# Batch row 0 of a conditional linear layer before a mixture of experts: loads in halves, another order of the first products and sums

## The chip, the cores and the metric

The kernel runs on one core of a Trainium2 chip. TensorE multiplies matrices, VectorE and ScalarE work elementwise and empty TensorE's result banks (PSUM), GpSimd (POOL) issues the indirect transfers, SyncE (SP) issues the direct ones. The metric is the device time of one execution in microseconds (us), less being better. Before the change it is 971.0 us, the median of three runs between 967.38 and 971.63.

## What is computed

For each of 4 batch rows of 1024 tokens, a linear layer is chosen by a category number. Its result goes through a router that sends each token to one of 8 experts, of 512 places each; each expert is a two-layer network with a ReLU; its output, times the router's probability, is added to x. All data are float32.

```python
def _L0_cond_ref(x, cat_ids, W, b):
    selected_W = W[cat_ids]
    selected_b = b[cat_ids]
    return jnp.einsum('bsd,bdh->bsh', x, selected_W) + selected_b[:, None, :]

def _L0_ffn_ref(x, Wr, W1, W2):
    ...
    probs = jax.nn.softmax(xf.astype(jnp.float32) @ Wr, axis=-1)
    eidx = jnp.argmax(probs, axis=-1)
    ...
    xe = xf[dispatch]
    h = jnp.maximum(jnp.einsum('ecd,edf->ecf', xe, W1), 0.0)
    ye = jnp.einsum('ecf,efd->ecd', h, W2)
    ye = ye * (pe * valid.astype(ye.dtype))[:, :, None]
    ...

x = x + _L0_ffn_ref(_L0_cond_ref(x, itok, W, b), Wr, W1, W2)
```

Here x is (4, 1024, 512), W (64, 512, 512), b (64, 512), Wr (512, 8), W1 (8, 512, 2048), W2 (8, 2048, 512).

## The kernel before

There are two stages. The first runs over the batch rows b = 0 to 3: the chosen linear layer and the router, whose results go to memory (`xc_dram`, and `slots` for the routing). The second runs over the experts, gathering rows by indirect transfers. The change touches the first stage alone, and in it only row 0.

A batch row is two chunks of 512 tokens (chunk c = 2b + g). Each chunk's product of a 512x512 matrix with the 512x512 weights is cut into 2x2 blocks and done with seven block products instead of eight (Strassen's way, as Winograd arranged the sums). The x blocks are called a11 to a22 and need the sums s1 to s4; the weight blocks b11 to b22 need t1 to t4. `linear(b, g, k)` (L400) does product k: 4 matmul instructions, which the trace shows as 8 records. k = 1 is a11 times b11, k = 2 a12 times b21, k = 6 is s2 times t2, 5 is s1 times t1, 7 is s3 times t3, 4 is a22 times t4, 3 is s4 times b22. Products 1, 6, 7 and 4 grow in one PSUM bank "x", which VectorE reads between them (`plus_bias`, L417, into the tiles s1, s6, s7), so that each next product of that bank waits for the reading of the one before.

Ahead of the products stand several helpers:

- `load_x` (L228) and `load_batch` (L193) issue the loads on SP: a chunk of x of 1 MB, the weights `cw` of 1 MB, the bias `cb` spread over the partitions, and the bias once more as columns, `cbt`. The category number is read into a register before (L194).
- `transpose_x` (X, L236) turns 128 rows of x by four TensorE transpositions; ScalarE copies the result from PSUM to `xT`. With a chunk's last rows it gives VectorE the four sums s1 to s4.
- `transpose_w` (WT, L260) does the same with a fourth of the weights into `wT`. These are for the router alone.
- `sum_w` (L221) gives VectorE the four differences t1 to t4.
- `through` (WM, L274) and `through_summed` (WS, L310) multiply the transposed weights with the router's matrix, giving `wrc`; `router` (R, L313) multiplies `xT` with `wrc`, `router_summed` (RS, L328) adds the parts; `choose` and `rank` pick the expert and the place.
- `keep_warm` (L65) issues matmuls on a tile of zeros, so that TensorE is active while loads run.

The order of TensorE and SP is written out by hand (`manual_schedule`): it is the order of the calls. For a row, `ORDER` (L455) lists the 14 products of the two chunks, and the tables `beside` (L463) and `loads` (L509) say which helpers follow each. The order of VectorE and ScalarE is chosen by a scheduler, except where `issue_after` (in `behind`, L73) puts an instruction behind the one kept in `latest`. Each engine works through its own list in order. PSUM for transpositions (`ps_t`) has two buffers.

The stage begins at L520: loads of three chunks of x and three rows' weights, six idle matmul instructions, four X, four WT, and then the loop over rows and products.

Of the kernel before, what the change touches and what calls it, by code (L numbers as in the profile page):

```python
# [11 lines left out]
ALU = mybir.AluOpType  # L12
# [4 lines left out]
P = 128  # L17
# [5 lines left out]
def kernel(  # L23
# [11 lines left out]
    nc = tc.nc  # L35
# [5 lines left out]
    KC = D // P  # L41
    NT = T // P
    GT = S // P
    XT = 4
    CT = XT * P
    HT = CT // 2
    SC = CAP // P
    HK = KC // 2
# [8 lines left out]
    xf = x.rearrange("b s d -> (b s) d")  # L57
# [7 lines left out]
    def keep_warm(pool, n):  # L65

        ps = pool.tile([P, D], F32, tag="t", name="ps_idle")
        for _ in range(n):
            nc.tensor.matmul(ps, lhsT=idle[:, 0:P], rhs=idle, start=True, stop=True)

    latest = [None]
# [6 lines left out]
    def unordered(group, ins):  # L78
# [14 lines left out]
        out=wr_sb[:, :, 0:E], in_=wr.rearrange("(kc p) e -> p kc e", p=P)  # L93
# [43 lines left out]
    banks = {}  # L137
# [40 lines left out]
    with (  # L178
# [14 lines left out]
        def load_batch(b):  # L193
            n = nc.sync.value_load(cat_sb[0:1, b : b + 1], min_val=0, max_val=NCAT - 1)  # L194
            w = cwp.tile([P, KC, D], F32, tag="cw", bufs=3, name=f"cw_{b}")
            nc.sync.dma_start(
                out=w,
                in_=cond_w[bass.ds(n, 1), :, :].rearrange("o (kc p) h -> p (o kc) h", p=P),
            )
            bias = cwp.tile([P, D], F32, tag="cb", bufs=3, name=f"cb_{b}")  # L200
            nc.sync.dma_start(
                out=bias, in_=cond_b[bass.ds(n, 1), :].to_broadcast([P, D])
            )
            bias_t = cwp.tile([P, KC], F32, tag="cbt", bufs=3, name=f"cbt_{b}")
            nc.sync.dma_start(
                out=bias_t, in_=cond_b[bass.ds(n, 1), :].rearrange("o (kc p) -> p (o kc)", p=P)
            )

            b11, b12, b21, b22 = (
                w[:, i * HK : (i + 1) * HK, j * HD : (j + 1) * HD]  # L210
                for i in range(2)
                for j in range(2)
            )
            wd = cwp.tile([P, 4, HK, HD], F32, tag="wd", name=f"wd_{b}")
            t1, t2, t3, t4 = (wd[:, k, :, :] for k in range(4))
            later_sums[b] = (b11, b12, b21, b22, t1, t2, t3, t4)
            cond[b] = (w, bias, bias_t, {1: b11, 2: b21, 3: b22, 4: t4, 5: t1, 6: t2, 7: t3})

        later_sums = {}
# [7 lines left out]

        def load_x(c):  # L228
            t = xin.tile([P, XT, D], F32, tag="x", name=f"x_{c}")
            nc.sync.dma_start(  # L230
                out=t,
                in_=xf[c * CT : (c + 1) * CT, :].rearrange("(j p) d -> p j d", p=P),
            )
            xrows[c] = t

        def transpose_x(b, i):  # L236


            c, j = b * 2 + i // XT, i % XT
            if j == 0:  # L240
                xT[c] = xtp.tile([P, KC, CT], F32, tag="xT", name=f"xT_{c}")
            ps = ps_t.tile([P, KC, P], F32, tag="t", name=f"ps_xT_{c}_{j}")
            for kc in range(KC):
                nc.tensor.transpose(ps[:, kc, :], xrows[c][:, j, kc * P : (kc + 1) * P], ident)
            nc.scalar.copy(xT[c][:, :, j * P : (j + 1) * P], ps)
            if j == XT - 1:
                a11, a12, a21, a22 = (
                    xT[c][:, k * HK : (k + 1) * HK, half * HT : (half + 1) * HT]
                    for half in range(2)
                    for k in range(2)  # L250
                )
                t = xsp.tile([P, 4, HK, HT], F32, tag="xs", name=f"xs_{c}")
                s1, s2, s3, s4 = (t[:, k, :, :] for k in range(4))
                nc.vector.tensor_tensor(s1, a21, a22, ALU.add)
                nc.vector.tensor_tensor(s2, s1, a11, ALU.subtract)
                nc.vector.tensor_tensor(s3, a11, a21, ALU.subtract)
                nc.vector.tensor_tensor(s4, a12, s2, ALU.subtract)
                xS[c] = {1: a11, 2: a12, 3: s4, 4: a22, 5: s1, 6: s2, 7: s3}

        def transpose_w(b, hc):  # L260
            if hc == 0:
                wT[b] = wtp.tile([P, KC, D], F32, tag="wT", name=f"wT_{b}")
            ps = ps_t.tile([P, KC, P], F32, tag="t", name=f"ps_wT_{b}_{hc}")
            for kc in range(KC):
                nc.tensor.transpose(
                    ps[:, kc, :], cond[b][0][:, kc, hc * P : (hc + 1) * P], ident
                )
            nc.scalar.copy(wT[b][:, hc, :].rearrange("p (k n) -> p k n", n=P), ps)
# [131 lines left out]
        def linear(b, g, k):  # L400

            key = ("lin", b, g)
            c = b * 2 + g
            ps = bank(ps_x, key, k, [P, 2, HD], "xc", bufs=2 if BANK[k] == "x" else 1)
            _, bias, _, right = cond[b]
            for j in range(2):
                for kc in range(HK):
                    nc.tensor.matmul(
                        ps[:, j, :],
                        lhsT=xS[c][k][:, kc, j * P : (j + 1) * P],  # L410
                        rhs=right[k][:, kc, :],
                        start=(k in OPENS and j == 0 and kc == 0),
                        stop=(k == LAST[BANK[k]] and j == 1 and kc == HK - 1),
                        skip_group_check=True,
                    )

            def plus_bias(into, half):  # L417
                nc.vector.tensor_tensor(
                    into,
                    ps,  # L420
                    bias[:, half * HD : (half + 1) * HD].unsqueeze(1).to_broadcast([P, 2, HD]),
                    ALU.add,
                )

            def block(i, j):
                return xco.tile([P, 2, HD], F32, tag=f"c{i}{j}", name=f"xc{i}{j}_{c}")

            def done(t, i, j):
                at = c * CT + i * HT
                nc.sync.dma_start(  # L430
                    out=xc_dram[at : at + HT, j * HD : (j + 1) * HD].rearrange(
                        "(j p) d -> p j d", p=P
                    ),
                    in_=t,
                )

            if k in (1, 6, 7):
                banks[key, k] = parts.tile([P, 2, HD], F32, tag=f"s{k}", name=f"s{k}_{b}_{g}")
                plus_bias(banks[key, k], 0 if k == 1 else 1)
            if k in (2, 3):  # L440
                t = block(0, int(k == 3))
                latest[0] = nc.vector.tensor_tensor(
                    t, ps, banks.pop((key, 1 if k == 2 else 6)), ALU.add
                )
                done(t, 0, int(k == 3))
            if k == 7:
                t = block(1, 1)
                nc.vector.tensor_tensor(t, banks[key, "y"], banks.pop((key, 7)), ALU.add)
                done(t, 1, 1)
            if k == 4:  # L450
                t = block(1, 0)
                plus_bias(t, 0)
                done(t, 1, 0)
# [5 lines left out]
        )  # L459

        X, WT, WM, WS = transpose_x, transpose_w, through, through_summed
        R, RS = router, router_summed
        beside = {  # L463
            (0, 0): [(sum_w, 0), (WM, 0)],
            (0, 1): [(X, 0, 4), (X, 0, 5), (WS, 0)],
            (0, 2): [(X, 0, 6), (X, 0, 7), (R, 0, 0)],
            (0, 3): [(WT, 1, 0)],
            (0, 4): [(WT, 1, 1), (RS, 0, 0)],
            (0, 5): [(WT, 1, 2), (R, 0, 1)],
            (0, 6): [(WT, 1, 3)],  # L470
            (0, 7): [(X, 1, 0), (WM, 1), (RS, 0, 1), (choose, 0)],
            (0, 8): [(X, 1, 1), (behind, sum_w, 1)],
# [47 lines left out]
        with tc.manual_schedule(engines={mybir.EngineType.PE, mybir.EngineType.SP}):  # L520
            load_x(0)
            load_batch(0)
            load_x(1)
            load_batch(1)
            load_x(2)
            load_batch(2)
            keep_warm(ps_t, 6)
            for i in range(XT):
                transpose_x(0, i)
            for hc in range(KC):  # L530
                transpose_w(0, hc)
            for b in range(B):
                for i, (g, k) in enumerate(ORDER):
                    linear(b, g, k)
                    for f, *at in loads.get((b, i), []) + beside.get((b, i), []):
                        f(*at)
            keep_warm(ps_t, 7)

        nc.scalar.dma_start(
            out=table.rearrange("p e c r -> p e (c r)"),  # L540
            in_=slots.rearrange("(e p c) r -> p e (c r)", e=E, c=SC),
# [237 lines left out]
```

## Time and profile before

| what | us |
|---|---|
| three runs: lowest, median, highest | 967.38, 971.0, 971.63 |
| the profiled execution: its time | 969.31 |
| its span, from first to last instruction | 967.5 |
| busy in the span: TensorE, VectorE, ScalarE, GpSimd | 950.1, 472.7, 171.0, 139.1 |
| first transposition of x on TensorE, from the span's start | 8.53 |
| first product on TensorE | 13.45 |
| idle matmuls at the end of the first stage begin | 153.27 |
| first transposition of the second stage | 160.80 |

Sections of the profile that are used here: the timeline gives, for a run of like instructions, the start and length in us, the engine, the line, output and inputs with their shapes, the number of records and in brackets the idle time before them and who ended it. PE is TensorE, PEld its weight loads, DVE VectorE, ACT ScalarE. A float32 matmul instruction shows as two records. The answer by windows gives for each stretch its length and each engine's busy time, then the granted clock of TensorE, the share of the DMA engines and the GB/s moved. The waits give an engine and line, whom it waited for, and the us in total, the times and the longest.

### The profile page before, as it was taken

Reading aid. Unit: us, or ns where it says so; the run is one execution under the profiler, and the core shown is the slowest. Engines: PE = TensorE matmul, PEld = TensorE weight load, DVE = VectorE, ACT = ScalarE, POOL = GpSimd, SP = SyncE. Lnnn points to the kernel's source line nnn. Section 1 sums busy time; section 2 is a strip of 40 time slices with the busy share of each in tenths; the row PEclk is TensorE's granted clock in tenths of the full one; section 3 lists DMA queues with packets and bytes.
Section 4 is the critical chain, followed back from the end, with each engine's and each line's share of the span. In section 5 each row is a group of like instructions: output and inputs, shape, how many; then the busy total and the mean of one; then the engine's idle time right before and its main releaser. Section 6 shows DMA issues by size and latency. Waiting matters only on the chain.

```text
span 967.5 us, 11249 instructions
## 1 busy us (share of the span) xinstructions
PE 950.1 (98%) x4570; PEld 812.2 (84%) x4570; DVE 472.7 (49%) x822; ACT 171.0 (18%) x289; POOL 139.1 (14%) x141
## 2 busy tenths in 40 slices
PE   9999988999999999999999999999999999999997
PEld 5788776888888888888888888888888888888886
DVE  4656574374337522762276317731673157325621
ACT  3233200320023002310231013101320132003200
POOL 0043332200022001200130013001300130012001
PEclk9999998999999999999999999999999999999999
DMA  9389223399134313532253225313532352332001
GB/s 323 115 166 227 90 81 93 132 400 337 60 131 159 131 55 114 173 107 74 84 175 127 82 93 174 130 48 128 174 101 73 127 174 71 104 126 87 1 0 44
DMA packets 95509, 123.18 MB, mean 127 GB/s; under 512 B 8820, under 2 KB 82548, under 8 KB 95266
## 3 DMA queue, kind: packets, MB, share of 16 engines
q1 hardware_dynamic: 85042, 97.54, 31.6%
q0 software_dynamic: 8704, 24.85, 7.8%
q8 instruction: 36, 0.59, 0.2%
q10 hardware_dynamic: 1712, 0.08, 0.1%
q14 instruction: 15, 0.12, 0.1%
HBM read 105.96 MB, written 25.23 MB: 136 GB/s over the span
## 4 chain that ended last, share of the span: by engine, by line
PE 58%; issue 17%; DVE 4%; DMA 2%; POOL 1%; SPq 1%; POOLq 0%; ACT 0%; DVEq 0%
PE hx L630 17%; PE yx L673 16%; PE yy L673 9%; PE hy L630 8%; PE hz L630 4%; PE yz L673 3%; DMA w_b<-in_L_ffn_W_dram 2%; PE ps_e L607 1%; POOL out_dram L694 1%; POOL rows L583 1%; SPq L566 1%; DMA rows<-xc_dram,src_row 0%; DVE h L150 0%; DVE h L151 0%; DVE h L149 0%
## 5 line engine op out<-in xcount | busy, mean ns | idle before, releaser
L630 PE MATMUL hx<-xe,w 128*128 128x256 f32 x1024 | 242.8, 382 | 1.4 <-ACT s L643 1.4
L630 PEld LDWEIGHTS hx<-xe,w 128*128 128x128 f32 x1024 | 195.3, 192 | 27.6 <-ACT s L643 1.8
L643 ACT COPY s<-hx 128x512 f32<-128x512 f32 x96 | 55.9, 582 | 437.7 <-PE hx L630 437.7
L630 PE MATMUL hy<-xe,w 128*128 128x256 f32 x512 | 122.1, 380 | 0.0
L673 PE MATMUL yx<-w_t,h 128*128 128x256 f32 x512 | 119.9, 380 | 1.2 <-DVE rows L667 1.2
L673 PE MATMUL yx<-w_b,h 128*128 128x256 f32 x512 | 116.6, 381 | 1.1 <-DVE rows L667 1.1
L694 POOL DMA_INDIRECT out_dram<-rows,dst_row x32 | 31.9, 998 | 572.1 <-DVE rows L667 572.1
L673 PEld LDWEIGHTS yx<-w_b,h 128*128 128x128 f32 x512 | 95.8, 190 | 16.5 <-DVE rows L667 3.7
L673 PEld LDWEIGHTS yx<-w_t,h 128*128 128x128 f32 x512 | 95.4, 190 | 15.9 <-DVE rows L667 2.0
L630 PEld LDWEIGHTS hy<-xe,w 128*128 128x128 f32 x512 | 97.4, 190 | 13.3 <-DVE h L646 0.4
L667 DVE SCALAR_TENSOR_TENSOR rows<-yx,table,rows 128x256 f32<-128x256 f32 x64 | 31.0, 484 | 140.2 <-PE yx L673 140.2
L647 ACT ACTIVATE h<-h 128x512 f32<-128x512 f32 x96 | 60.5, 630 | 203.0 <-DVE h L646 203.0
L646 DVE TENSOR_TENSOR h<-hy,s 128x512 f32<-128x512 f32 x64 | 44.2, 691 | 98.8 <-PE hy L630 54.8
L630 PE MATMUL hz<-xe,w 128*128 128x256 f32 x256 | 61.7, 380 | 0.0
L673 PE MATMUL yz<-w_b,h 128*128 128x256 f32 x256 | 58.7, 383 | 0.4
L673 PE MATMUL yy<-w_b,h 128*128 128x256 f32 x256 | 58.4, 381 | 0.0
L673 PE MATMUL yy<-w_t,h 128*128 128x256 f32 x256 | 57.9, 380 | 0.0
L583 POOL DMA_INDIRECT rows<-in_x_dram,at x32 | 40.2, 1257 | 122.7 <-DVE at L594 93.0
L673 PEld LDWEIGHTS yz<-w_b,h 128*128 128x128 f32 x256 | 48.1, 190 | 9.5 <-DVE rows L667 3.4
L630 PEld LDWEIGHTS hz<-xe,w 128*128 128x128 f32 x256 | 48.9, 191 | 6.6
L673 PEld LDWEIGHTS yy<-w_b,h 128*128 128x128 f32 x256 | 47.6, 190 | 8.1 <-DVE rows L667 1.4
L673 PEld LDWEIGHTS yy<-w_t,h 128*128 128x128 f32 x256 | 48.2, 190 | 6.2
(118 smaller groups left out, 894.7 us busy)
## 6 DMA issues: line engine op xcount, KB each, us to landing
w<-in_L_ffn_W_dram SPq DMA_DIRECT2D x64, 512.0 KB, 4.3
w_b<-in_L_ffn_W_dram SPq DMA_DIRECT2D x32, 1024.0 KB, 5.5
x<-in_x_dram SPq DMA_DIRECT2D x8, 1024.0 KB, 9.7
xc_dram<-xc SPq DMA_DIRECT2D x32, 256.0 KB, 4.1
out_dram<-in_x_dram SPq DMA_DIRECT2D x2, 2816.0 KB, 22.4
cw<-in_L_cond_W_dram SPq DMA_DIRECT2D x4, 1024.0 KB, 11.2
out_dram<-in_x_dram SPq DMA_DIRECT2D x1, 2560.0 KB, 16.0
cb<-in_L_cond_b_dram SPq DMA_DIRECT2D x4, 256.0 KB, 9.9
```

Source lines behind the costliest of these rows:

```text
L566: nc.sync.dma_start(out=t[k], in_=w2[e, i * F // 2 : (i + 1) * F // 2, j * D // 2 : (j + 1) * D // 2].rearrange("(m p) d -> p m d", p=P),)
L583: nc.gpsimd.indirect_dma_start(out=into[n], out_offset=None, in_=source, in_offset=bass.IndirectOffsetOnAxis(ap=at[:, c : c + 1], axis=0),)
L607: nc.tensor.transpose(ps[:, kc, :], r[:, kc * P : (kc + 1) * P], ident)
L630: nc.tensor.matmul(ps[:, j, :], lhsT=w1s[e, g][:, LEFT[k], kc, j * P : (j + 1) * P], rhs=xes[e][:, RIGHT1[k], kc, :], start=(k in OPENS an ...
L643: nc.scalar.copy(banks[key, k], ps)
L646: latest[0] = nc.vector.tensor_tensor(into, ps, part, ALU.add)
L647: nc.scalar.activation(into, into, AF.Relu)
L667: nc.vector.scalar_tensor_tensor(row, ps[:, at, :], table[:, e, half * HC + at, 0:1], row, ALU.mult, ALU.add)
L673: nc.tensor.matmul(ps[:, at, :], lhsT=hs[e, m // HB][:, LEFT[k], m % HB, at * P : (at + 1) * P], rhs=w2s[e][RIGHT2[k]][:, m, :], start=(k ...
L694: nc.gpsimd.indirect_dma_start(out=of, out_offset=bass.IndirectOffsetOnAxis(ap=dst_row[:, n : n + 1], axis=0), in_=residual.pop(n), in_off ...
```

## The change

For chunk 0, x is loaded by two transfers of 512 KB each, and for row 0 so are the weights; all other loads stay whole. Three idle matmul instructions are issued instead of six. Row 0's four WT leave their place ahead of the loop and stand behind its first and second product; the helpers that followed the products 0 to 5 of row 0 are spread anew. VectorE's eight sums of chunk 0 get an order by hand: s1, t1, s2, t2, then the reading of product 1's bank, then s3, t3, s4, t4 (`rest_of_first`). For this, `plus_bias` returns its instruction, and `latest` is also set behind product 1. From product 4 of chunk 0 on (index 6 of the order), TensorE's list is the one before, and the lists of the other engines are so from about there on.

```diff
--- before.py
+++ after.py
@@ -193,10 +193,14 @@
         def load_batch(b):
             n = nc.sync.value_load(cat_sb[0:1, b : b + 1], min_val=0, max_val=NCAT - 1)
             w = cwp.tile([P, KC, D], F32, tag="cw", bufs=3, name=f"cw_{b}")
-            nc.sync.dma_start(
-                out=w,
-                in_=cond_w[bass.ds(n, 1), :, :].rearrange("o (kc p) h -> p (o kc) h", p=P),
-            )
+            kcs = [(0, HK), (HK, KC)] if b == 0 else [(0, KC)]
+            for i, (lo, hi) in enumerate(kcs):
+                nc.sync.dma_start(
+                    out=w[:, lo:hi, :],
+                    in_=cond_w[bass.ds(n, 1), lo * P : hi * P, :].rearrange(
+                        "o (kc p) h -> p (o kc) h", p=P
+                    ),
+                )
             bias = cwp.tile([P, D], F32, tag="cb", bufs=3, name=f"cb_{b}")
             nc.sync.dma_start(
                 out=bias, in_=cond_b[bass.ds(n, 1), :].to_broadcast([P, D])
@@ -227,11 +231,23 @@
 
         def load_x(c):
             t = xin.tile([P, XT, D], F32, tag="x", name=f"x_{c}")
-            nc.sync.dma_start(
-                out=t,
-                in_=xf[c * CT : (c + 1) * CT, :].rearrange("(j p) d -> p j d", p=P),
-            )
+            n = XT // 2 if c == 0 else XT
+            for j in range(0, XT, n):
+                nc.sync.dma_start(
+                    out=t[:, j : j + n, :],
+                    in_=xf[c * CT + j * P : c * CT + (j + n) * P, :].rearrange(
+                        "(j p) d -> p j d", p=P
+                    ),
+                )
             xrows[c] = t
+
+        def behind_this(f):
+            with tc.issue_after(latest[0].ins):
+                latest[0] = f()
+
+        def rest_of_first():
+            for f in later_sums.pop("rest"):
+                behind_this(f)
 
         def transpose_x(b, i):
 
@@ -251,10 +267,28 @@
                 )
                 t = xsp.tile([P, 4, HK, HT], F32, tag="xs", name=f"xs_{c}")
                 s1, s2, s3, s4 = (t[:, k, :, :] for k in range(4))
-                nc.vector.tensor_tensor(s1, a21, a22, ALU.add)
-                nc.vector.tensor_tensor(s2, s1, a11, ALU.subtract)
-                nc.vector.tensor_tensor(s3, a11, a21, ALU.subtract)
-                nc.vector.tensor_tensor(s4, a12, s2, ALU.subtract)
+                tt = nc.vector.tensor_tensor
+                todo = [
+                    lambda: tt(s1, a21, a22, ALU.add),
+                    lambda: tt(s2, s1, a11, ALU.subtract),
+                    lambda: tt(s3, a11, a21, ALU.subtract),
+                    lambda: tt(s4, a12, s2, ALU.subtract),
+                ]
+                if c == 0:
+
+                    b11, b12, b21, b22, t1, t2, t3, t4 = later_sums.pop(0)
+                    todo[1:1] = [lambda: tt(t1, b12, b11, ALU.subtract)]
+                    todo[3:3] = [lambda: tt(t2, b22, t1, ALU.subtract)]
+                    todo[5:5] = [lambda: tt(t3, b22, b12, ALU.subtract)]
+                    todo[7:7] = [lambda: tt(t4, b21, t2, ALU.subtract)]
+                    rest = todo[4:]
+                    latest[0] = todo[0]()
+                    for f in todo[1:4]:
+                        behind_this(f)
+                    later_sums["rest"] = rest
+                else:
+                    for f in todo:
+                        f()
                 xS[c] = {1: a11, 2: a12, 3: s4, 4: a22, 5: s1, 6: s2, 7: s3}
 
         def transpose_w(b, hc):
@@ -415,7 +449,7 @@
                     )
 
             def plus_bias(into, half):
-                nc.vector.tensor_tensor(
+                return nc.vector.tensor_tensor(
                     into,
                     ps,
                     bias[:, half * HD : (half + 1) * HD].unsqueeze(1).to_broadcast([P, 2, HD]),
@@ -436,7 +470,9 @@
 
             if k in (1, 6, 7):
                 banks[key, k] = parts.tile([P, 2, HD], F32, tag=f"s{k}", name=f"s{k}_{b}_{g}")
-                plus_bias(banks[key, k], 0 if k == 1 else 1)
+                evicted = plus_bias(banks[key, k], 0 if k == 1 else 1)
+                if k == 1:
+                    latest[0] = evicted
             if k in (2, 3):
                 t = block(0, int(k == 3))
                 latest[0] = nc.vector.tensor_tensor(
@@ -461,12 +497,12 @@
         X, WT, WM, WS = transpose_x, transpose_w, through, through_summed
         R, RS = router, router_summed
         beside = {
-            (0, 0): [(sum_w, 0), (WM, 0)],
-            (0, 1): [(X, 0, 4), (X, 0, 5), (WS, 0)],
-            (0, 2): [(X, 0, 6), (X, 0, 7), (R, 0, 0)],
-            (0, 3): [(WT, 1, 0)],
-            (0, 4): [(WT, 1, 1), (RS, 0, 0)],
-            (0, 5): [(WT, 1, 2), (R, 0, 1)],
+            (0, 0): [(rest_of_first,), (WT, 0, 0), (WT, 0, 1)],
+            (0, 1): [(WT, 0, 2), (WT, 0, 3)],
+            (0, 2): [(WM, 0), (X, 0, 4), (X, 0, 5)],
+            (0, 3): [(X, 0, 6), (WS, 0), (X, 0, 7)],
+            (0, 4): [(R, 0, 0), (WT, 1, 0), (WT, 1, 1)],
+            (0, 5): [(R, 0, 1), (WT, 1, 2), (RS, 0, 0)],
             (0, 6): [(WT, 1, 3)],
             (0, 7): [(X, 1, 0), (WM, 1), (RS, 0, 1), (choose, 0)],
             (0, 8): [(X, 1, 1), (behind, sum_w, 1)],
@@ -524,11 +560,9 @@
             load_batch(1)
             load_x(2)
             load_batch(2)
-            keep_warm(ps_t, 6)
+            keep_warm(ps_t, 3)
             for i in range(XT):
                 transpose_x(0, i)
-            for hc in range(KC):
-                transpose_w(0, hc)
             for b in range(B):
                 for i, (g, k) in enumerate(ORDER):
                     linear(b, g, k)
```

## The prediction

> **What bounds the kernel now.** I read the page first. TensorE is busy 98% of 967.5 us and the chain that ended last is mostly PE; the expert loop, four fifths of the span, is not touched. So I went to the only place where the change acts, the first 35 us, in the timeline of TensorE, to see when its useful work starts and where it stalls.
>
> ```profile
> 1.45 7.24 PE L69 MATMUL ps_idle<-idle 128*128 128x512 f32 x12 [1.45 <-DVE idle L89]
> ...
> 8.53 1.04 PE L244 MATMUL ps_xT<-ident,x 128*128 128x128 f32 x8
> 9.80 1.14 PE L244 MATMUL ps_xT<-ident,x 128*128 128x128 f32 x8 [0.24 <-ACT xT L245]
> 11.13 1.15 PE L265 MATMUL ps_wT<-ident,cw 128*128 128x128 f32 x8 [0.19 <-ACT xT L245]
> 12.46 1.15 PE L265 MATMUL ps_wT<-ident,cw 128*128 128x128 f32 x8 [0.18 <-ACT wT L268]
> ...
> 28.00 1.89 PE L408 MATMUL xcx_lin<-cw,xT 128*128 128x256 f32 x8
> 29.73 0.60 PE L265 MATMUL ps_wT<-ident,cw 128*128 128x128 f32 x4
> 30.26 1.06 PE L317 MATMUL ps_lT<-xT,wrc 128*32 128x512 f32 x8
> 31.26 2.00 PE L408 MATMUL xcx_lin<-wd,xT 128*128 128x256 f32 x8
> ```
>
> The reader sees three things. Twelve idle matmul records (six instructions, two records each) hold TensorE until 8.53. Then 32 transposition records run in groups of eight, 1.27 to 1.33 us apart, because each group waits for ScalarE to empty a bank; the same four-instruction transposition between products takes 0.44 to 0.53 (29.73 to 30.26). From 13.45, where the first product starts, TensorE has no gap up to 31.26, where product 4 of the first chunk starts (index 6 of the order). That start is my measuring mark: both kernels have done the same set of work by then.
>
> Next, when the operands land: the answer by tile, narrowed to one issue each, for x and then for the weights cw, with issue lengths in ns, first and last start in us, and the time from issue to landing.
>
> ```profile
> L230 SPq DMA_DIRECT2D x<-in_x_dram x1: 422/422/422, 1.1 to 1.1; - x1
> ...
> DMA to landing us min/median/max: 5.9/5.9/5.9
> ```
>
> ```profile
> L196 SPq DMA_DIRECT2D cw<-in_L_cond_W_dram x1: 392/392/392, 2.9 to 2.9; - x1
> ...
> DMA to landing us min/median/max: 7.2/7.2/7.2
> ```
>
> x is issued at 1.14 and lands at about 7.0, 1.5 us before TensorE turns to it: the idle matmuls, not x, set the start. The weights, issued at 2.92, land at 10.1; VectorE's first sum starts at 10.12 and confirms it. The windows of the same time show how fast the bytes come (last two columns: share of the DMA engines and GB/s):
>
> ```profile
> 4.00:6.00 2.00, 2.00 (x5) 0.83 (x4) 0.00 (x0) 0.00 (x0) 0.00 (x0) 1.00 1.01 314
> 6.00:8.00 2.00, 2.00 (x6) 0.91 (x5) 0.00 (x0) 0.00 (x0) 0.00 (x0) 1.00 1.02 307
> 8.00:10.00 2.00, 1.76 (x12) 1.14 (x11) 0.00 (x0) 0.84 (x2) 0.00 (x0) 1.00 0.98 367
> ```
>
> The DMA engines are full; halves come sooner only because they stand first in line. Last, the waits of TensorE over 0 to 170 us:
>
> ```profile
> PE ps_e L607 <- DMA rows<-xc_dram,src_row: 2.5, 3, 1.4
> PE xcx_lin L408 <- DVE s L418: 1.5, 1, 1.5
> PE ps_idle L69 <- DVE idle L89: 1.5, 1, 1.5
> PE rk L375 <- DVE past L356: 1.5, 1, 1.5
> ```
>
> Nothing there waits for a load from memory except the gathers at 160 us, which themselves follow the last product. So whatever the start gains runs through to the end.
>
> **What the Trainium skill says.** "TensorE: Matmul & The Clock Gate", Part 1: the clock is halved until about 3.4 us of activity have passed, and falls again after an idle window. The trace agrees: weight loads of idle matmuls stand 0.85 us apart until 5.03 and 0.43 afterwards, 3.6 us after the first. Part 4 says that transpositions don't count as activity; here the trace differs: 4.9 us of nothing else (8.53 to 13.45) did not cool the clock, as the next products run at 0.22 us per record. "DMA: Bandwidth & Descriptors", Queues, rings and completion order: each DMA engine takes descriptors in ring order; the trace agrees (x at 7.0, cw at 10.1, the second x at 4.78 + 9.0 = 13.8, in order of issue). The same page, on why a DMA increments its semaphore by 16: only the full count says that data has landed, so half a tile can be used early only as a transfer of its own. No run here shows that yet.
>
> **The change part by part.**
>
> Three idle instructions fewer: 6 records x 0.43 = 2.58 us. The idle work ends at 8.53 - 2.58 = 5.95, if the first half of x is there. Half of x is 0.52 MB, 1.67 us at 314 GB/s, so it lands near 7.0 - 1.7 = 5.4. Bounds: 4.5 to 6.5; I take 5.4, no wait.
>
> x transpositions: chunk rows 0 and 1 from 5.95; rows 2 and 3 from 5.95 + 1.27 = 7.22, which both the ScalarE copy and the second half of x (7.0, with the extra issue perhaps 7.4) allow. TensorE is free at about 8.2 to 8.4.
>
> First product: needs only the upper half of cw. 0.52 MB at 367 GB/s is 1.43 us, so it lands at 10.12 - 1.43 = 8.7; I take 8.8 for the second x issue ahead of it. TensorE waits about 0.5 us. Bounds: 8.2 (TensorE free) and 10.1 (halves land together).
>
> The weight transpositions move from ahead of the first product to behind the first two. Four groups at 0.5 in the flow are 2.0 us. The path from first product to mark was 31.26 - 13.45 = 17.81; now it is 17.81 + 2.0 = 19.8. The mark comes at 8.8 + 19.8 = 28.6, against 31.26: **2.6 us gained**. Bounds: 3.2 from 8.2, 1.3 from 10.1. The router steps only change places between the same products, their sum stays.
>
> VectorE in order of use: its eight sums, 0.6 to 0.72 us apart, are the same eight. s1 starts when the fourth copy of xT ends (5.95 + 3.03 = 9.0), t1 at 9.6, s2 at 10.3, t2 at 10.9 (second half of cw at about 10.2), eviction of product 1 at 11.6 to 12.3. Product 6 needs t2, s2 and that eviction; it stands at 8.8 + 1.8 + 0.9 + 1.8 + 0.9 = 14.2. Cover: 1.9 us, and beyond that each us of lateness costs one. The other four sums (12.3 to 15) sit behind the eviction by hand; product 7 needs s3 and t3 only near 21. The first result block's addition waits to about 15; its store is waited for by the next chunk's block at about 40. So the order costs nothing but is what lets product 6 follow; s3 and t3 ahead of the eviction would have eaten 1.3 of the cover.
>
> SP issues two more transfers, 0.42 and 0.39 us and some register work: the bias goes out up to 1.0 later and lands by 10.7 + 1.0 = 11.7, about when the eviction reaches it. The second x lands by 14.8 instead of 13.8, used at about 17; the second cw is issued at 6.22 and the slowest of the first three took 11.8, so 19 at the latest, used by TensorE near 24. Covered by 2 and 5 us. No DMA volume is added.
>
> Sum against the profiled execution: 969.3 (967.5 of span and 1.8 around it) - 2.6 = 966.7. The runs shown have their median at 971.0, 1.7 higher; scaled to them, 971.0 - 2.6 = **968.4 us**, 0.27% less. What a measurement here can tell from no change is about 0.5%, 4.9 us: the expected gain is real but below it.
>
> **The rivals.**
>
> Halves land together. For it: the DMA engines are full from 4 us, and two transfers interleaved finish near each other. Against: ring order above. Gain 1.3, or 0.4 if the extra issue adds 0.9: 970.1.
>
> Gain and luck at the stage boundary. Between 162.4 and 168.8 the windows show the granted clock at 0.50: the gap before the gathers cools TensorE. If the shift changes which window that gap falls in, up to 3 us more go: 968.4 - 3 = 965.4, which would read as faster. Nothing says that it does; the runs before differ by 4.3 us, so something of this size varies anyway.
>
> A cold clock at the start, the slower side. Where: the wait ahead of the first product at 8.4. With three idle instructions less, transpositions that leave gaps and a wait of 0.5 to 1.7 us, TensorE could fall to half clock. Price from the boundary: 6.4 us at 0.50, 3.2 us lost. From the likely gain that gives 971.0 - 2.6 + 3.2 = 971.6; with halves together (gain 0.4), 973.8. It decides once the lost time exceeds 2.6: over 5.2 us at half clock. Against it: the 4.9 us of transpositions with gaps of 0.2 that stayed warm. Passing 0.5% slower needs two such stretches or a first half of cw after 16 us.
>
> The gain doesn't arrive: DMA stays full until 28 us in absolute time, so a load waited for then would hold TensorE to the old clock time. Covers of 2 to 5 us speak against it. 971.0.
>
> **How the numbers follow.** Forecast 0.62; halves together 0.15; boundary luck 0.12; cold start 0.08; nothing arrives 0.03. Faster by over 0.5%: the luck case and a little of the forecast's edge, 0.14. Slower by over 0.5%: the worse half of the cold start, 0.04. Same: 0.82. The range runs from 965.0 (luck) to 971.5 (nothing gained or a cold start at its usual price), leaving out under 2 in 10.
>
> **What would show it.** Right: TensorE's first x transposition near 6.0, the first product near 8.8 with a short wait, no wait of product 6 for VectorE, and the mark (product 4 of chunk 0) near 28.6; the last idle matmuls of the conditional stage then begin 2.6 us sooner than 153.27. Wrong: the first product after 10; a TensorE wait on VectorE between 12 and 25; products spaced 0.43 per record before 20 us; or a mark at 28.6 with the end of the stage where it was.

## The result, and the profile after

Six runs of the changed kernel lie between 965.1 and 967.78 us, median 966.1; six of the kernel before have their median at 970.9. The ratio is 0.9957, with a 95% interval of 0.9938 to 0.9975: 4.2 us faster (2.4 to 6.0), where 2.6 were forecast; the two medians are 4.9 apart. The time stands inside the range given. The profiled execution took 965.1 us with a span of 963.3, against 969.3 and 967.5.

The timeline of TensorE in the kernel after, the lines that answer to those of before (start, length, line, what, records, and in brackets the idle time before and who ended it):

```profile
1.45 4.75 PE L69 MATMUL ps_idle<-idle 128*128 128x512 f32 x6 [1.45 <-DVE idle L89]
6.03 1.04 PE L260 MATMUL ps_xT<-ident,x 128*128 128x128 f32 x8
7.31 1.15 PE L260 MATMUL ps_xT<-ident,x 128*128 128x128 f32 x8 [0.24 <-ACT xT L261]
8.97 1.99 PE L442 MATMUL xcx_lin<-cw,xT 128*128 128x256 f32 x8 [0.51 <-DMA cw<-in_L_cond_W_dram]
10.80 1.04 PE L299 MATMUL ps_wT<-ident,cw 128*128 128x128 f32 x8
11.67 1.89 PE L442 MATMUL xcz_lin<-cw,xT 128*128 128x256 f32 x8
13.40 1.04 PE L299 MATMUL ps_wT<-ident,cw 128*128 128x128 f32 x8
14.27 1.89 PE L442 MATMUL xcx_lin<-wd,xs 128*128 128x256 f32 x8
...
28.59 1.89 PE L442 MATMUL xcx_lin<-wd,xT 128*128 128x256 f32 x8
```

The first product starts at 8.97 instead of 13.45, the weights' four transpositions stand behind the first two products (two in each row of 8 records), and the mark (the last line) comes at 28.59 instead of 31.26. The only wait on a load in these lines is the 0.51 ahead of the first product. The third product of the list (k = 6, at 14.27) follows without a wait for VectorE, whose own timeline shows why: s1, t1, s2 and t2 are done at 11.6 and the reading of the first bank at 12.2.

```profile
9.11 0.69 DVE L272 TENSOR_TENSOR xs<-xT 128x512 f32<-128x512 f32 x1 [6.61 <-ACT xT L261]
9.72 0.68 DVE L280 TENSOR_TENSOR wd<-cw 128x512 f32<-128x512 f32 x1
10.32 0.69 DVE L273 TENSOR_TENSOR xs<-xs,xT 128x512 f32<-128x512 f32 x1
10.92 0.69 DVE L281 TENSOR_TENSOR wd<-cw,wd 128x512 f32<-128x512 f32 x1
11.52 0.69 DVE L452 TENSOR_TENSOR s<-xcx_lin,cb 128x512 f32<-128x512 f32 x1
```

How the gain then travels, from the timelines of the two profiled executions. In the second stage hx, hy and hz are the PSUM banks of an expert's first layer, yx and yz those of its second; w1 and w2 are the weights of the two layers (w and w_b in the traces). The stretch between the end of the first stage and the first product hz, in which TensorE waits for gathered rows, is called the gap below.

| moment, us from the span's start | before | after | gained by then |
|---|---|---|---|
| mark, product 4 of chunk 0 | 31.26 | 28.59 | 2.67 |
| idle matmuls at the end of the first stage | 153.27 | 150.50 | 2.77 |
| first transposition of gathered rows | 160.80 | 157.97 | 2.83 |
| first product hz of expert 0 | 168.90 | 163.88 | 5.02 |
| first product yx of expert 0 | 214.03 | 209.84 | 4.19 |
| end of the span | 967.5 | 963.3 | 4.2 |

The start gives 2.7 and keeps them for 130 us. Then 2.2 more come inside the gap, between the first gathered transposition and hz (8.1 us apart before, 5.9 after), and 0.8 are given back by yx. The windows of the gap start where the idle matmuls end, at 159.44 and 156.67; first the kernel before, then after (the last three columns are the granted clock of TensorE, the share of the DMA engines and GB/s):

```profile
159.44:163.44 4.00, 1.77 (x9) 1.13 (x8) 0.69 (x1) 0.00 (x0) 2.11 (x3) 0.84 0.68 202
163.44:167.44 4.00, 3.69 (x13) 3.25 (x14) 2.21 (x4) 0.00 (x0) 0.00 (x0) 0.50 0.12 46
```

```profile
156.67:160.67 4.00, 1.31 (x9) 0.84 (x8) 1.12 (x2) 0.00 (x0) 2.00 (x3) 1.00 0.69 197
160.67:164.67 4.00, 3.61 (x20) 3.04 (x21) 2.76 (x5) 0.58 (x1) 0.00 (x0) 1.00 0.13 49
```

Waiting for the gathered rows left TensorE idle for more than half of the first four microseconds in both, yet the clock fell to half in one and stayed in the other, which was idle for longer. What was given back is in the waits of TensorE from 160 to 225 us, in the kernel after:

```profile
PE hx L664 <- ACT s L677: 1.4, 1, 1.4
PE ps_e L641 <- DMA rows<-xc_dram,src_row: 0.9, 2, 0.7
PE hy L664 <- DVE h L680: 0.7, 1, 0.7
PE yx L707 <- DVE rows L701: 0.5, 1, 0.5
```

The wait of hy is new. The kernel before has the 1.4 and the 0.5 as well. VectorE's timeline says what stands behind the new one; the first line is of the kernel before, the other two of the kernel after:

```profile
203.48 1.23 DVE L156 TENSOR_TENSOR w_t<-w_b,w_b 128x1024 f32<-128x1024 f32 x1 [2.80 <-DMA w_b<-in_L_ffn_W_dram]
...
199.29 1.23 DVE L156 TENSOR_TENSOR w_t<-w_b,w_b 128x1024 f32<-128x1024 f32 x1 [3.53 <-DMA w_b<-in_L_ffn_W_dram]
200.44 0.68 DVE L680 TENSOR_TENSOR h<-hy,s 128x512 f32<-128x512 f32 x1
```

A sum of w2 blocks waits 3.53 for its load, and the sum h that empties TensorE's bank is queued behind it. SP had issued these loads only at 179.06, behind a load of w1 that itself waits for a buffer. In the kernel before they went out at 183.97, so the issue moved forward by 4.9, nearly as much as TensorE; but the sum that needs them moved by only 4.2. The loads took 0.7 longer, and why is open.

### The profile page after: what moved, and what is told of

Read it like the earlier page. It is cut to its first block, busy times and chain, and to the rows that moved or that the text cites. A ratio compares the mean times of both kernels' runs of the same rounds, so it can differ in the third digit from the quotient of the medians.

```text
span 963.3 us, 11240 instructions
## 1 busy us (share of the span) xinstructions
PE 944.5 (98%) x4564; PEld 807.2 (84%) x4564; DVE 471.9 (49%) x822; ACT 170.7 (18%) x289; POOL 140.3 (15%) x141
## 4 chain that ended last, share of the span: by engine, by line
PE 58%; issue 17%; DVE 4%; DMA 2%; POOL 1%; SPq 0%; POOLq 0%; ACT 0%; DVEq 0%
PE hx L664 17%; PE yx L707 16%; PE yy L707 9%; PE hy L664 8%; PE hz L664 4%; PE yz L707 3%; DMA w_b<-in_L_ffn_W_dram 2%; PE ps_e L641 1%; POOL out_dram L728 1%; POOL rows L617 1%; SPq L600 0%; DMA rows<-xc_dram,src_row 0%; DVE h L151 0%; DVE h L150 0%; DVE h L149 0%
## 6 DMA issues: line engine op xcount, KB each, us to landing
cw<-in_L_cond_W_dram SPq DMA_DIRECT2D x3, 1024.0 KB, 11.6
```

## The experiments

My theory was that the start is worth what was forecast (halves and fewer idle instructions together), that the rest of the measured gain is the clock in the gap, and that the first expert's w2 loads take part of it back. The rivals: the gain is the gap's alone; one part of the change does all; the order of the sums matters; fewer idle instructions cool the start. "Clock lost" below is worked out from each run's record: one minus the mean granted clock, times the span, averaged over the runs. It bounds what a cool clock cost, since cool time in which TensorE waits anyway costs nothing. It is rough: the clock is on record in steps of 0.001, about 1 us each, and the slow idle matmuls of the first 5 us are not in it, as the windows there show 1.00.

**The gap kept warm, in both kernels.** Eight idle instructions instead of seven end the stage, and one more stands ahead of each of two transposition groups:

```diff
-            keep_warm(ps_t, 7)
+            keep_warm(ps_t, 8)
...
+        if e == 0 and c in (1, 2):
+            w = D if c == 1 else HD
+            nc.tensor.matmul(
+                ps.rearrange("p k n -> p (k n)")[:, 0:w],
+                lhsT=idle[:, 0:P],
+                rhs=idle[:, 0:w],
+                start=True,
+                stop=True,
+            )
```

The kernel before with this edit:

> The kernel before, with TensorE kept active through the gap between the two stages: eight idle instructions instead of seven at the stage's end, and one more idle matmul ahead of the second and third group of gathered rows. Theory A (the gap cools TensorE's clock in the kernel before, and a part of the gain came from its not cooling in the changed kernel): granted clock 1.00 from 158 to 170 us, the first hz product near 166 instead of 168.90, about 0.7 of it given back to the wait for the first expert's second-layer weights, time near 968.5, and a narrower spread. Rival B (the clock at the gap is noise and the gain is all from the start): time within 0.5 of before.

The kernel after with it:

> The changed kernel with the same idle matmuls in the gap. Theory A: it was warm already in its profile, so its time stays within 1 us of the changed kernel's 966.1, and stands 2.7 us below the kernel before with the gap filled. Rival B: it stands 4.9 below that one.

Measured: before warmed 968.9 (ratio to before 0.999, 0.9983 to 0.9997), after warmed 965.8 (0.9958, 0.9944 to 0.9971). So with the same edit to the gap in both, the change is still worth 3.2 us, and their marks stand at 30.93 and 28.89, 2.0 apart: the gain is not the gap's alone. (In the two profiles it is 2.9 at hz and 2.4 at the end.) Clock lost fell from 3.3 us (59 runs of before) to 0.9 (22 runs), but the time only by 1.0, and in the changed kernel from 2.4 to 0.8 with no gain in the ratio that the intervals could show. TensorE's wait of hy is 0.4 in the first and 1.0 in the second: part of what the clock frees, the wait for w2 takes back.

**Idle instructions alone.** The kernel before with three instead of six, and the kernel after with six instead of three:

```diff
-            keep_warm(ps_t, 6)
+            keep_warm(ps_t, 3)
```

```diff
-            keep_warm(ps_t, 3)
+            keep_warm(ps_t, 6)
```

> The kernel before with three idle instructions at the start instead of six, nothing else. If the idle matmuls alone were in the way, product 4 of chunk 0 starts near 31.26 - 2.6 = 28.7. My own sum: x lands at 7.0, its transpositions end near 9.5, the weights land at 10.1 and only then are transposed, so the first product starts near 12.7 and product 4 of chunk 0 near 30.5: 0.8 gained.

> The changed kernel with six idle instructions at the start again. My sum: x transpositions from 8.6, first product near 11.0 without a wait for the weights, product 4 of chunk 0 near 30.6 against 28.59: 2.0 of the 2.7 lost. If the order and the halves were what gained, not the earlier start, it stays below 29.5.

Measured: before with three 968.9 (0.9988, 0.9981 to 0.9996), mark at 30.83; after with six 968.6 (0.9987, 0.998 to 0.9994), mark at 30.17. The starts, first of the kernel before with three, then of the kernel after with six:

```profile
6.86 1.45 PE L244 MATMUL ps_xT<-ident,x 128*128 128x128 f32 x8
8.54 1.14 PE L244 MATMUL ps_xT<-ident,x 128*128 128x128 f32 x8 [0.24 <-ACT xT L245]
10.74 1.07 PE L265 MATMUL ps_wT<-ident,cw 128*128 128x128 f32 x8 [1.05 <-DMA cw<-in_L_cond_W_dram]
```

```profile
8.39 1.04 PE L260 MATMUL ps_xT<-ident,x 128*128 128x128 f32 x8
...
10.65 1.89 PE L442 MATMUL xcx_lin<-cw,xT 128*128 128x256 f32 x8
```

Neither part is the change. Three idle instructions less bring the mark 0.43 forward by themselves: the weights land too late for more, and a wait of 1.05 takes the place of the idle work. Halves and the new order alone bring 1.09. Together they bring 2.67.

The same two profiles say something of the gap. Its windows, from the end of the idle matmuls on, again first the kernel before with three idle instructions, then the kernel after with six:

```profile
159.00:163.00 4.00, 1.31 (x9) 0.84 (x8) 1.01 (x2) 0.00 (x0) 2.25 (x3) 1.00 0.73 198
163.00:167.00 4.00, 3.33 (x19) 2.78 (x20) 2.60 (x5) 0.31 (x1) 0.00 (x0) 1.00 0.15 52
```

```profile
158.24:162.24 4.00, 1.32 (x9) 0.84 (x8) 1.25 (x2) 0.00 (x0) 2.00 (x3) 0.96 0.69 204
162.24:166.24 4.00, 3.85 (x16) 3.45 (x17) 1.80 (x4) 0.00 (x0) 0.00 (x0) 0.62 0.10 40
```

Here it is the kernel before that kept its clock and a form of the kernel after that lost it, with the same busy time in the first window as in the kernel after (1.31). So neither the change nor the share of idle time decides whether the clock falls in one execution.

**Halves undone.** The kernel after with whole loads, all else kept:

```diff
-            kcs = [(0, HK), (HK, KC)] if b == 0 else [(0, KC)]
+            kcs = [(0, KC)]
...
-            n = XT // 2 if c == 0 else XT
+            n = XT
```

> The changed kernel with x and the weights of row 0 loaded whole; order, sums and idle matmuls as changed. My sum: x lands at 7.0 and the weights at 10.1, so the first product starts near 10.2 instead of 8.97 and product 4 of chunk 0 near 29.9: 1.3 lost, about half of the gain. If the halves land together anyway, as the rival had it, nothing is lost.

Measured: 967.3 (0.9969, 0.9956 to 0.9981), mark at 30.22, 1.6 later than with halves and 1.0 sooner than in the kernel before. So of the 2.67, idle instructions alone bring 0.43, moving the weights' transpositions behind the first products adds 0.6 to that, and the halves 1.6; the order in which the parts are added sets their shares. TensorE waits 0.91 for x and 1.17 for the weights:

```profile
6.98 1.06 PE L260 MATMUL ps_xT<-ident,x 128*128 128x128 f32 x8 [0.91 <-DMA x<-in_x_dram]
8.29 1.14 PE L260 MATMUL ps_xT<-ident,x 128*128 128x128 f32 x8 [0.24 <-ACT xT L261]
10.60 1.99 PE L442 MATMUL xcx_lin<-cw,xT 128*128 128x256 f32 x8 [1.17 <-DMA cw<-in_L_cond_W_dram]
```

**The order of the sums undone.** The kernel after with VectorE's order left to the scheduler:

```diff
-                if c == 0:
...
-                else:
-                    for f in todo:
-                        f()
+                for f in todo:
+                    f()
...
-            (0, 0): [(rest_of_first,), (WT, 0, 0), (WT, 0, 1)],
+            (0, 0): [(sum_w, 0), (WT, 0, 0), (WT, 0, 1)],
```

> The changed kernel with the eight sums of chunk 0 left to the scheduler, which lists t1 to t4 first, then s1, s3, s2, then the reading of product 1's bank. My sum: t1 at 9.0, t2 at 10.1 when the second half of the weights is there, then one each 0.6 us, so that bank is read from 13.7 to 14.4; product 6 could start at 14.27, so 0.2 to 0.5 is lost at that place and no more. If the order by hand carries the gain, more than 1 us is lost.

Measured: 965.2 (0.9946, 0.993 to 0.9963), mark at 28.80. The scheduler put t1 to t4 first, then the s sums, of which s4 alone came after the reading of the first bank, at 13.64 instead of 11.52. Product 6 started at 14.38, but in this execution the first product had started 0.20 sooner, at 8.77. From the first product to the mark it took 20.03, against 19.62 in the kernel after: by these two profiles the hand order is worth 0.4, inside the 0.2 to 0.5 expected. In time no run tells it from nothing.

**One idle instruction.** The kernel after with the least idle work, to provoke a cold start:

```diff
-            keep_warm(ps_t, 3)
+            keep_warm(ps_t, 1)
```

> The changed kernel with one idle instruction instead of three, as a test of the cold start. x transpositions start when the first half of x lands, at 5.0. Theory cold: the clock isn't released by transpositions and short work, the first products run at 0.43 us per record for a window, product 4 of chunk 0 comes near 31 or later. Rival: transpositions count as activity, products at 0.22, the first product still at 9.0 because it waits for the weights, product 4 of chunk 0 at 28.6, no change in time.

Measured: 966.8 (0.9963, 0.9949 to 0.9976), mark at 28.23.

```profile
1.45 2.07 PE L69 MATMUL ps_idle<-idle 128*128 128x512 f32 x2 [1.45 <-DVE idle L89]
5.05 3.38 PE L260 MATMUL ps_xT<-ident,x 128*128 128x128 f32 x16 [1.52 <-DMA x<-in_x_dram]
8.61 1.99 PE L442 MATMUL xcx_lin<-cw,xT 128*128 128x256 f32 x8 [0.17 <-DMA cw<-in_L_cond_W_dram]
```

The transpositions run slowly (16 records in 3.38, against 2.43 from 6.03 to 8.46 in the kernel after), but x is there at 5.05, and the products from 8.61 on go at full pace, 8 records in 1.99. No product started cold.

**w2 loads earlier, free and held back.** In the kernel after, `load_w2(0)` moves from the second group of expert 0 to the first, ahead of a load of w1 that waits for a buffer:

```diff
+                if e == 0 and g == 0:
+                    load_w2(0)
                 if g > 0:
                     first_layer(e, g - 1, 4)
...
-                    if g == 1:
-                        load_w2(0)
```

> The changed kernel with the first expert's second-layer weights loaded from the start of the second stage, ahead of the wait for a buffer that held SP from 151 to 178. If the 0.7 us that went missing between 170 and 205 us was the wait for these weights, the product at 201 has no wait for VectorE any more, and 0.7 to 2.6 is gained (the two other waits of TensorE up to 215, 1.4 and 0.5, may go as well). If it was something else, the time stays.

Measured: 966.1 (0.9948, 0.9932 to 0.9963). The waits behind the gap are gone, but the loads go out at 151.76, ahead of the gathers, and the rows come late. The waits of TensorE from 150 to 175:

```profile
PE ps_e L641 <- DMA rows<-xc_dram,src_row: 5.3, 2, 4.7
```

The clock falls to 0.50 in 162 to 166, hz starts 4.8 later than in the kernel after, and yx only 2.0 later. So 2.8 vanished behind the gap and 4.8 appeared in it. That the loads slowed the gathers is in their own times: issued at 154.65 and after, as in the kernel after (154.46), they landed 6.2 to 6.6 us after their issue instead of 3.5 to 3.7. The held version adds to this edit a copy that a w2 buffer must wait for, after the gathered rows have been transposed:

```diff
+        if e == 0:
+            nc.vector.tensor_copy(t["b11"][:, 0, 0:2], xes[0][:, 6, 0, 0:2])
```

> The changed kernel with the first expert's second-layer weights loaded early, but only after the gathered rows have been transposed (VectorE writes two elements of the first weight tile then, so that its load waits for that). Loaded early without that, they took the memory path from the gathers and TensorE waited 4.7 us for them, and won as much back later. If both halves of that reading hold: no wait for the gathers beyond the 1.3 of the changed kernel, none of the three waits between 200 and 215, 2 to 4 us gained over the changed kernel. If the early weights only moved waits about: no gain.

It ran beside the kernel after, unchanged, on the same chip:

> The changed kernel itself, unaltered, beside the two that follow. If the start is worth 2.7 and the gap on average 1, it stands 3.5 to 4 below the kernel before; if the first comparison's 4.9 was the rule, 4.9.

Measured: held 966.4 (0.9934, 0.9918 to 0.9949), unchanged 967.9 (0.9951, 0.9937 to 0.9965), which is 4.6 below the kernel before by the medians. Held is 1.4 below unchanged, less than the 2 to 4 expected, and the intervals overlap. Held loads are issued at 171.4, and TensorE has no wait between the gap and 225. It waited 2.9 in all for the gathered rows, much as in the kernel after (3.1), but in this execution the clock fell with it, to 0.76 over 158 to 172, and hz started 16.0 after the end of the stage instead of 13.4. Both profiles show a second, new stall: ScalarE's `part` (L359) waits 2.2 until 109 us for something the profile can only call "remote", and TensorE then waits 2.4 (unchanged) and 1.7 (held) near 113. The stage ended 4.6 and 2.0 later than in the first profile of the kernel after. What it is stays open; the next version, from the same chip, has 1.0 of the same wait of TensorE without that of ScalarE. The start is not behind it: the marks are at 28.77 and 28.60, as elsewhere.

**All of it, with the halves reordered.** Warm gap, held w2, and on SP first half of x, first half of the weights, second half of x, second half of the weights, with the first product ahead of the transposition of rows 2 and 3:

```diff
-            load_x(0)
+            load_x(0, 0)
...
+                if b == 0 and i == 0:
+                    load_x(0, 1)
...
+                if i == 1:
+                    linear(0, 0, 1)
```

> As the last, with TensorE kept active in the gap, and with the halves loaded in the order x, weights, x, weights and the first product ahead of the second two x transpositions, since it reads only the first halves. The first product then starts near 7.2 without a wait, product 4 of chunk 0 near 28.1 (the second half of the weights, at 10.2, sets the next step): 0.5 more at the start, and a narrower spread; 962 to 963 in all. If the waits for loads only move, it equals the last.

Measured: 965.8 (0.9939, 0.9924 to 0.9953) where 962 to 963 was expected, the mark at 30.14 where 28.1 was expected. The first half of the weights, now second in line, came no sooner:

```profile
6.73 1.40 PE L263 MATMUL ps_xT<-ident,x 128*128 128x128 f32 x8
9.16 1.97 PE L447 MATMUL xcx_lin<-cw,xT 128*128 128x256 f32 x8 [1.02 <-DMA cw<-in_L_cond_W_dram]
10.96 1.04 PE L263 MATMUL ps_xT<-ident,x 128*128 128x128 f32 x8
```

The mark is 1.55 later than in the kernel after: 0.2 because the first product starts later, and the rest because the transposition of rows 2 and 3, which used to be done before the weights came, now stands between the products. The window from 2 us to the first product says why the weights came no sooner:

```profile
2.00:9.16 7.16, 6.14 (x15) 2.77 (x13) 0.50 (x6) 2.36 (x3) 0.01 (x1) 1.00 0.89 292
```

292 GB/s over 7.16 us are 2.1 MB, twice the 1.05 MB of the two halves at the head of the line. The later transfers were served beside them. In the kernel after it was 2.2 MB from 2 us to 8.97, with 1.6 MB at the head.

**The start as the change made it, warm gap and held w2.** The two edits shown above, without the reordered halves.

> The changed kernel with both remedies for the stretch behind the first stage (an idle matmul ahead of the gathered rows' transpositions of chunks 1 and 2, and the first expert's w2 loads issued early but held back by a VectorE copy until those rows are transposed), and with the start left as the change made it. Main theory: the start keeps its 2.7 us (mark at 28.6 to 28.9), the gap keeps its clock (first product of the gathered rows 13.4 to 13.8 us after the end of the stage), and the wait of 0.7 to 1.0 us for the sum h is gone; a ratio to before of 0.993 to 0.995, about 0.5 to 1 us better than the change alone. Rival (the held loads cost the gap what they save behind it, as the held loads alone did when rows arrived 2.9 us late and the clock fell to 0.76): ratio 0.995 to 0.996, no better than the change.

Measured: 962.5 us, 962.1 to 962.9 in five runs, against 969.7 of before; ratio 0.9921 (0.9907 to 0.9934), better than the 0.993 to 0.995 expected. This beats both kernels: its interval lies below those of the kernel after (0.9938 to 0.9975 and 0.9937 to 0.9965), though barely, and the kernel after was not run beside it on this chip. Mark 28.88, end of stage 150.77, hz at 165.06, yx at 208.2, span 961.1. The windows of its gap, and SP's issue and VectorE's use of w2:

```profile
158.00:162.00 4.00, 2.83 (x15) 1.76 (x16) 1.38 (x2) 0.00 (x0) 1.74 (x2) 1.00 0.65 196
162.00:166.00 4.00, 3.40 (x20) 2.88 (x19) 3.09 (x5) 0.58 (x1) 0.00 (x0) 1.00 0.02 8
```

```profile
167.99 5.43 SPq L602 DMA_DIRECT2D w_b<-in_L_ffn_W_dram  x4
```

```profile
192.37 1.22 DVE L156 TENSOR_TENSOR w_t<-w_b,w_b 128x1024 f32<-128x1024 f32 x1
```

The loads go out 11 us sooner than in the kernel after, once the gathers are through; VectorE's first sum of w2 waits for nothing; TensorE has no wait from 165 to 225. From hz to yx it takes 43.2 us, against 46.0 in the kernel after: 2.8 less. The gap takes 0.9 more than in that profile, which had kept its clock, and the mark is 0.3 later; yx comes 1.6 sooner and the span is 2.2 shorter. Neither edit alone came as low (0.9958 and 0.9934), but the interval of held w2 alone overlaps with this one. The profiles show why both may be needed: warm without held w2 still has the wait of hy, 1.0, and held w2 without warm lost its clock. Clock lost is 1.0 here and 3.2 with held w2 alone. Whether the two edits by themselves, on the kernel before, would bring the same was not tried.

## Why the prediction was right, and where it was off

**The start: right in mechanism and size.** First x transposition forecast near 6.0, seen at 6.03; first product 8.8 with a wait of about 0.5, seen 8.97 with 0.51; product 6 at 14.2, seen 14.27, no wait; mark 28.6, seen 28.59. That the mark fits to 0.01 is luck: the first product came 0.17 later than forecast, and the way from it to the mark was 0.2 shorter, because the four moved transpositions cost 1.81 (19.62 against 17.81) where 2.0 was put. In the six profiles with this start the first product lies between 8.84 and 9.34, and the way to the mark between 19.55 and 19.63: what varies is when the weights land and the idle work ends. VectorE's moments are 9.11, 9.72, 10.32, 10.92 and 11.52, as forecast to about 0.1. The stage's end came 2.77 sooner: nothing on the way took the gain back. That the idle work and not x sets the start held for before. It was half the truth: the run with three idle instructions alone shows the weights right behind, so the 2.58 of idle work is worth 0.43 with nothing else changed.

**"Halves come sooner only because they stand first in line": too simple.** The halves landed at about 5.0 and 6.4 (x; forecast 5.4 and 7.0) and 8.9 and 10.2 (weights; forecast 8.8 and 10.2). But the reordered run shows that standing earlier brought nothing, and the bytes moved show transfers served together. The forecast of 8.8 was met by a model that would have been wrong for the next step. The prediction cited the Trainium skill, "DMA: Bandwidth & Descriptors", Queues, rings and completion order, for ring order; the same section warns that completion is still not first in, first out for an issuing engine. The runs fit that warning so far as bytes of later transfers moved before an earlier one was usable (2.1 MB against 1.05); whether a later one also finished first, they do not show. The rival of halves landing together fell: 1.3 us lay between the two halves of the weights, and whole loads cost 1.6 at the mark.

**Order of the sums: "the order costs nothing" held.** "Eaten 1.3 of the cover" was not tested by itself. Undone, three sums that product 6 does not need stood ahead of the reading, which came 2.1 later; the cover of 1.9 was used up, and the way to the mark grew by 0.4.

**"So whatever the start gains runs through to the end": the step that was mis-sized.** It is right for the first stage and wrong as a sum of 2.6 for the whole. Behind the stage the gain changed twice, by +2.2 (clock in the gap) and -0.8 (new wait for w2). The clock was priced as luck, up to 3 us at a chance of 0.12. The 2.2 is also the luck of which executions were profiled, as the kernel before with three idle instructions kept its clock and four forms of the kernel after lost theirs (six idle instructions, whole loads, the scheduler's order, held w2). Over the runs it is less: clock lost averages 2.4 us in the first six runs of the kernel after, and 2.8 to 3.8 in the four groups of runs of before, so 0.4 to 1.4 us of the 4.2 can be clock. With 2.0 to 2.7 from the start that makes 2.4 to 4.1, and the remainder lies inside the interval. Whether the clock really holds more often after the change was not settled: the gap's contents are the same, and only its place moved.

**w2 was not seen.** The list of waits was read to 170 us, where it ended with the gathers; the chain of the kernel before, read only for its PE share, named the loads of w2. By engine and by line:

```profile
PE 58%; issue 17%; DVE 4%; DMA 2%; POOL 1%; SPq 1%; POOLq 0%; ACT 0%; DVEq 0%
PE hx L630 17%; PE yx L673 16%; PE yy L673 9%; PE hy L630 8%; PE hz L630 4%; PE yz L673 3%; DMA w_b<-in_L_ffn_W_dram 2%; PE ps_e L607 1%; POOL out_dram L694 1%; POOL rows L583 1%; SPq L566 1%; DMA rows<-xc_dram,src_row 0%; DVE h L150 0%; DVE h L151 0%; DVE h L149 0%
```

In the best version, with both remedies, the line by engine reads:

```profile
PE 61%; issue 17%; DVE 3%; POOL 1%; DMA 0%; POOLq 0%
```

**The cold start: rightly held unlikely.** Even one idle instruction did not bring it to the products; only the transpositions ran slowly.

## What to carry to other kernels

When two things arrive almost together (idle work ending and a load landing), removing one buys only the distance to the other: price the pair, and test each part alone before crediting it. Follow a gain past the stage in which it is made to the next load that is tied to something else, here w2, which waits on SP's queue behind a load that needs a buffer; of the 5.0 us gained by hz, 0.8 was lost there, and moving that load won 2.8 between hz and yx. A load moved earlier needs a gate of its own if a transfer that sets the path is still to come. Compare windows of two executions from the same event on, not at the same clock time, and take more than one profile before a cool clock is put down to a change.

## What the runs showed of the hardware that was not expected

- The same gap cooled the clock in some executions and not in others: with 1.31 or 1.32 us busy in the first four after the idle work, it stayed at 1.00 in the kernel after and in the kernel before with three idle instructions, and fell in the kernel after with six (0.62 in the next four). The Trainium skill, "TensorE: Matmul & The Clock Gate", Part 1, says that the activity window runs freely and so the moment of a change varies by about 0.5 us from run to run. At the start that agrees: the same six idle records took between 4.4 and 5.5 us in the runs of the two kernels' variants. For the gap it is a guess that the same thing decides; no run shows it.
- Two idle records and then 16 transposition records, 3.38 us of them, were enough for products at full pace at 8.61. Nothing but transpositions ran on TensorE from 5.05 to 8.43.
- Four loads of 1 MB, issued ahead of the gathers, made TensorE's longest wait for gathered rows 4.7 us, against 1.3 in the kernel after. The skill's "DMA: Bandwidth & Descriptors", Queues, rings and completion order, says that a DMA engine takes turns between the queues it has work for; here that did not keep the gathers at their pace beside a full queue of large loads, as they landed 6.2 to 6.6 us after their issue instead of 3.5 to 3.7.
